# P1 of the feed-forward residual as seven smaller products in its own PSUM bank

## The chip, the cores and the metric

The kernel runs on one core of one Trainium2 chip. The metric is the device time of one execution in microseconds, as the median of several runs; lower is better. All numbers are fp32.

## The reference

A conditioned transformer block: two residual branches, each with a layer norm that is scaled and shifted by a vector of the condition, and gated by another. The tokens are 2 batches of 2048 with 512 features. The change lies in the last product, `hf @ ff_w2`.

```python
emb = jnp.dot(jax.nn.silu(t), ada_w) + ada_b
shift_msa, scale_msa, gate_msa, shift_mlp, scale_mlp, gate_mlp = jnp.split(emb, 6, axis=-1)
norm = _ln(x) * (1.0 + scale_msa[:, None]) + shift_msa[:, None]
h = jax.nn.gelu(jnp.dot(norm, ssm_w1) + ssm_b1, approximate=False)
ssm_out = jnp.dot(h, ssm_w2) + ssm_b2
x = x + gate_msa[:, None] * ssm_out
norm2 = _ln(x) * (1.0 + scale_mlp[:, None]) + shift_mlp[:, None]
hf = jax.nn.gelu(jnp.dot(norm2, ff_w1) + ff_b1, approximate=True)   # 512 -> 1024
ff_out = jnp.dot(hf, ff_w2) + ff_b2                                 # 1024 -> 512
x = x + gate_mlp[:, None] * ff_out
```

## The kernel before

The 4096 tokens are worked in 8 blocks of 512. First come the norms and the first branch (`ssm1`, `ssm2`) for all blocks, then the second branch in four pairs of blocks: `ff1` for a pair, then `ff2` for its two blocks one after the other. `weight_fw2(b)` prepares the second weight of the feed-forward for batch b: it loads it, multiplies it by the batch's gate and makes the combinations that the fast products need. It runs for batch 0 during the first branch and for batch 1 during the `ff1` of the third pair.

Every large product is done by the Strassen-Winograd scheme: a product of 2 by 2 quarters takes seven products, named P1 to P7, in place of eight. `first` and `second` make the operands of one side: four additions or subtractions (s0, s1, an in-place q21 or q12, and s2), and then P1 and P2 use quarters as they are, P5 uses s0, P6 uses s1, P7 the in-place one. In `ff2` the scheme is used twice. Of the seven outer products, P2, P3, P4, P5 and P7 are split again: each has seven inner products, which the code calls leaves. P1 and P6 are done whole by `plain`: 8 matmuls of 128 by 128 by 256 each, with 4 steps over the contraction.

The order on TensorE in one `ff2` block is written out: `plain("P1")`; then seven rounds over the inner products in the order of `LEAVES` (P1, P2, P6, P5, P7, P3, P4), each round one leaf of each of the five split products (10 matmuls of 128 by 128 by 128); `plain("P6")` stands between the first and the second round. Both plain products add up in one PSUM bank, `Y_SEED` (bank 2), which ScalarE seeds with the bias row (`seed`). VectorE adds PSUM results into `xt`, the block's residual rows, which are then stored. The leaves add up in banks of their own (`ROOMS`). Banks of name "y" are used by inner P1, P6, P7, P4, "x" by P2, "v" by P5 and P3; after round 0 ScalarE copies the "y" results to "x" (the room copies).

The code does not issue instructions directly. Each helper (`mm`, `tt`, `copy`, `act`, `dma`) adds an operation to `Plan`. `Plan.order` keeps TensorE's order as written, works back from it to the latest time at which each other operation is due, and lets a list scheduler choose the order on VectorE, ScalarE, GpSimd and the DMA queue; an operation marked "vg" may go to VectorE or GpSimd. It counts a PSUM bank as one cell: a write to a bank waits for all earlier reads of it by other engines.

Lines in the profile: L294 is the matmul of `mm`, L256 `tt` (all additions), L283 `copy`, L274 `act`, L316 the issue of a DMA. Names of tiles: `hidden` holds the gelu output (the token side of `ff2`), `near` and `far` the sums for the first and the second block of a pair, `fw` (fw2) the second weight and its combinations, `gb` the bias row times the gate, `rows` the residual rows, `ring` and `turned` the operands of `ff1`.

```python
LEAVES = ("P1", "P2", "P6", "P5", "P7", "P3", "P4")
LEAF_AT = {"P1": (0, 0), "P2": (0, 0), "P6": (0, 1), "P5": (1, 1), "P7": (1, 1), "P3": (0, 1), "P4": (1, 0)}
Y_SEED, V_SEED = 2, 1
ROOMS = {("P23", "y"): 0, ("P23", "x"): 3, ("P23", "v"): 4, ("P4", "y"): 5, ("P4", "x"): 6, ("P4", "v"): 7}
```

Of the kernel before, what the change touches and what calls it, by code (L numbers as in the profile page):

```python
# [12 lines left out]
ALU = mybir.AluOpType  # L13
# [185 lines left out]
def kernel(  # L199
# [17 lines left out]
    P = 128  # L217
# [33 lines left out]
    def tt(e, o, a, b, f):  # L251
        n, ps = cols(o), in_psum(a, b)
        cost = {"v": n / 0.96 + 70, "g": 2.12 * n + 145}
        plan.add(
            e,
            lambda E: E.tensor_tensor(o, a, b, f),  # L256
            [o],
            [a, b],
            cost,
            {"v": cost["v"] + 85, "g": cost["g"] + 45},  # L260
            "g" if ps else "vg",
        )
# [64 lines left out]
    def region(name, kb):  # L327
        t = const.tile([P, kb * 256], F32, tag=name, name=name)
        scratch.add(t.tensor.name)
        return t  # L330

    def kept(name, *shape):
        t = const.tile([P, *shape], F32, tag=name, name=name)
        scratch.add(t.tensor.name)
        return t
# [6 lines left out]
    def kb(t, at, n):  # L342
        return t[:, at * 256 : (at + n) * 256]

    def cut(t, form, **sizes):
        return t.rearrange(form, **sizes)

    turned_r, ring_r, hidden_r = region("turned", 28), region("ring", 27), region("hidden", 32)
    near_r, far_r, rows_r = region("near", 27), region("far", 27), region("rows", 16)
    fw2_r = region("fw2", 43)  # L350

    banks = []
    for n in range(8):
# [34 lines left out]
    gate_rows = {g: kb(hidden_r, 29, 1)[:, n * P : (n + 1) * P] for n, g in enumerate((2, 5))}  # L388
    gb2 = [kb(ring_r, 22, 2), kb(ring_r, 24, 2)]
    gate_sb = kb(near_r, 22, 2)  # L390
    gb5 = [kept(f"gb5_{b}", D) for b in range(B)]
    leaf_row = kept("leaf_row", 3, P)
    cols_t = kept("cols", 64)
    mods = {g: kept(f"mod_{g}", KD, B) for g in (0, 1, 3, 4)}
    half_t = kept("half", C)
    marks = [kept(f"marks_{n}", 60) for n in range(4)]
# [9 lines left out]
    def thirds(t):  # L406
        return [t[:, n] for n in range(3)]

    def first(q, s, e="vg", cuts=1):
        parts(e, s[0], q["21"], q["22"], ALU.add, cuts)  # L410
        parts(e, s[1], s[0], q["11"], ALU.subtract, cuts)
        parts(e, q["21"], q["11"], q["21"], ALU.subtract, cuts)
        parts(e, s[2], q["12"], s[1], ALU.subtract, cuts)
        return {"P1": q["11"], "P2": q["12"], "P3": s[2], "P4": q["22"], "P5": s[0], "P6": s[1], "P7": q["21"]}

    def second(q, s, e="vg", cuts=1):
# [6 lines left out]
    def parts(e, o, a, b, f, cuts):  # L423
        n = o.shape[1] // cuts
        for r in [slice(c * n, (c + 1) * n) for c in range(cuts)]:
            tt(e, o[:, r], a[:, r], b[:, r], f)
# [63 lines left out]
    def gate_bias(t, g_ps, row):  # L490
        load_row(t, row)
        tt("v", t, g_ps, t, ALU.mult)
        tt("vg", t[:, D // 2 :], t[:, D // 2 :], t[:, : D // 2], ALU.subtract)
# [218 lines left out]
    def seed(bank, row, part):  # L712
        half = row[:, part * (D // 2) : (part + 1) * (D // 2)]
        copy(pair(bank), half.unsqueeze(1).to_broadcast([P, 2, HT]))
# [66 lines left out]

    fw2_t = cut(kb(fw2_r, 0, 16), "p (k d) -> p k d", k=KH)
    fw2_s = cut(kb(fw2_r, 16, 12), "p (s k d) -> p s k d", s=3, k=KH // 2)
    fw2_l = cut(kb(fw2_r, 28, 15), "p (a s k d) -> p a s k d", a=5, s=3, k=2)

    def fw2_operands(make):
        first_level = lambda q, s, **kw: second(q, s, **kw) if make else second_names(q, s)

        wops = first_level(quarters_of_second(fw2_t, KH), thirds(fw2_s), cuts=2)
        pair_t = cut(kb(fw2_r, 28, 6), "p (s k q d) -> p s k q d", s=3, k=2, q=2)  # L790

        def views(w):
            v = cut(w, "p (h k) (q e d) -> p h k q e d", h=2, e=2, d=P)
            return {f"{h + 1}{e + 1}": v[:, h, :, :, e, :] for h in range(2) for e in range(2)}

        o23 = first_level(views(fw2_t[:, KH // 2 :, :]), thirds(pair_t))
        leaves = {p: {n: v[:, :, j, :] for n, v in o23.items()} for j, p in enumerate(("P2", "P3"))}
        lo12 = fw2_t[:, : KH // 2, D // 2 :]
        for j, (p, w) in enumerate((("P4", fw2_s[:, 2]), ("P5", fw2_s[:, 0]), ("P7", lo12))):
            q = {n: v[:, :, 0, :] for n, v in views(w).items()}  # L800
            leaves[p] = first_level(q, thirds(fw2_l[:, 2 + j]))
        return wops, leaves
# [4 lines left out]
    def weight_fw2(b, bank):  # L807
        plan.stage = f"weight_fw2 {b}"
        src = fw2.rearrange("(o n t p) d -> n o p t d", o=2, n=2, p=P)
        for n in range(2):  # L810
            for o in range(2):
                dma(fw2_t[:, 4 * n + 2 * o : 4 * n + 2 * o + 2], src[n, o], lead=100000.0)
        g = gate(5, b, bank)
        gate_bias(gb5[b], g, fb2)
        for k in range(KH):
            tt("v" if bank else "vg", fw2_t[:, k, :], fw2_t[:, k, :], g, ALU.mult)
        return fw2_operands(True)
# [122 lines left out]
    def ff2(s, blk, wops, leaf_wops):  # L940
# [3 lines left out]
        xt, F = x1_t[blk], D // 2  # L944
        for c in range(C):
            dma(xt[:, c], x1_d[i][:, c])
        row = gb5[i // PER_B]
        lo, hi = hC[:, blk, 0], hC[:, blk, 1]
        sums = cut(kb(sums_r[blk], 0, 12), "p (g s k t) -> p g s k t", g=2, s=3, k=2)
        hops = {}  # L950
        for g in range(2):
            r = slice(2 * g, 2 * g + 2)
            q = {"11": lo[:, r, :HT], "12": hi[:, r, :HT], "21": lo[:, r, HT:], "22": hi[:, r, HT:]}
            hops[g] = first(q, thirds(sums[:, g]))
        WL = 2 * P
        leaf_r = kb(sums_r[blk], 12, 15)
        r24, r35 = leaf_r[:, : 6 * WL], leaf_r[:, 6 * WL : 12 * WL]
        r7 = [leaf_r[:, (12 + n) * WL : (13 + n) * WL] for n in range(3)]
        hi_v = cut(hi, "p (g k) (q e t) -> p g k q e t", g=2, q=2, e=2)
        lo_v = cut(lo, "p (g k) (q e t) -> p g k q e t", g=2, q=2, e=2)  # L960
        eg = [(e, g, f"{e + 1}{g + 1}") for e in range(2) for g in range(2)]
        q24 = {n: hi_v[:, g, :, :, e, :] for e, g, n in eg}
        q35 = {n: sums[:, g, 0:3:2, :, e * P : (e + 1) * P] for e, g, n in eg}
        q7 = {n: lo_v[:, g, :, 1, e, :] for e, g, n in eg}
        o24 = first(q24, thirds(cut(r24, "p (s k q t) -> p s k q t", s=3, k=2, q=2)))
        o35 = first(q35, thirds(cut(r35, "p (s n k t) -> p s n k t", s=3, n=2, k=2)))
        o7 = first(q7, [cut(r, "p (k t) -> p k t", k=2) for r in r7])
        leaves = {
# [2 lines left out]
            "P3": {n: o[:, 1] for n, o in o35.items()},  # L971
            "P5": {n: o[:, 0] for n, o in o35.items()},
            "P7": o7,
        }

        seed(Y_SEED, row, 0)
        copy(banks[V_SEED][:, :P], row[:, F : F + P])
        tt("vg", leaf_row[:, 2], row[:, F + P :], row[:, F : F + P], ALU.subtract)
        quad_v = cut(banks[ROOMS["P4", "v"]], "p (n d) -> p n d", d=P)
        copy(quad_v[:, :3, :], leaf_row)  # L980

# [2 lines left out]
        def plain(p):  # L984
            for j in range(2):
                for k in range(KH // 2):
                    mm(
                        pair(Y_SEED)[:, j, :],
                        hops[k // 2][p][:, k % 2, j * P : (j + 1) * P],
                        wops[p][:, k, :],  # L990
                        False,
                        k == KH // 2 - 1,
                    )
# [22 lines left out]
                a = a.unsqueeze(1).to_broadcast(list(d.shape))  # L1016
            tt("v", d, a, d, ALU.add)

        plain("P1")
        add(xt[:, 0:2, :F], pair(Y_SEED))  # L1020
        for r, f in enumerate(LEAVES):
            t, e = LEAF_AT[f]
            on = ("P4", "P7", "P2", "P3", "P5") if last and r == 6 else ("P2", "P3", "P5", "P4", "P7")
            done = {p: leaf(p, f) for p in on}
            if r == 0:
                copy(rooms["P23", "x"][:, :2], rooms["P23", "y"][:, :2])
                copy(rooms["P4", "x"][:, :2], rooms["P4", "y"][:, :2])
                copy(rooms["P4", "x"][:, 2], seeded[:, 0])
                started.update({("P23", "x"), ("P4", "x")})
                plain("P6")  # L1030
                continue
            dests = {
                "P3": (X[:, 0, t, :, e, :], rooms["P23", BANK[f]][:, :2, :]),
                "P5": (X[:, :, t, 1, e, :], done["P5"]),
                "P4": (X[:, 1, t, 0, e, :], done["P4"]),
                "P7": (X[:, 1, t, :, e, :], done["P7"]),
            }
            for p in on:
                if p in dests:
                    add(*dests[p])  # L1040
            if r == 1:
                add(xt[:, 0:2, F:], pair(Y_SEED))
            if r == 2:
                d = cut(xt[:, 2:4, :], "p t (q d) -> p t q d", q=2)
                tt("v", d, pair(Y_SEED).unsqueeze(2).to_broadcast([P, 2, 2, F]), d, ALU.add)
            if last and r >= 4:
                for row_t in (t, 2 + t):
                    q = "sa"[row_t // 2]
                    if f == "P3":
                        dma(out_blk[i][:, row_t, :], xt[:, row_t, :], q)  # L1050
                    else:
                        cs = slice(e * P, (e + 1) * P)
                        dma(
                            out_blk[i][:, row_t].rearrange("p (q d) -> p q d", q=2)[:, :, cs],
                            cut(xt[:, row_t], "p (q d) -> p q d", q=2)[:, :, cs],
                            q,
                        )
# [210 lines left out]
```

## Time and profile before

| | |
|---|---|
| median of 3 runs | 572.83 us (572.78 to 573.93) |
| the profiled execution | 572.99 us |
| its span, first to last instruction | 571.2 us |
| granted TensorE clock | 0.999 |
| the four `ff1` stages begin at about | 216, 303, 391, 479 us |
| the `ff2` blocks of the four pairs begin at about | 257.9, 345.6, 434.2, 521.9 us |

PE is TensorE's matmuls and PEld its weight loads, DVE is VectorE, ACT ScalarE, POOL GpSimd. A timeline row gives the start, the length, engine and line, the operation, the tile written and the tiles read, the shape and the count of merged instructions, and in brackets the engine's idle time before it with what ended that. A row of a chain gives start, length and what worked. A row of groups ends with the busy time and the mean length in ns. Lengths of matmuls overlap, so the distance between starts is what a matmul takes.

### The profile page before, as it was taken

Reading aid. Unit: us, or ns where it says so; the run is one execution under the profiler, and the core shown is the slowest. Engines: PE = TensorE matmul, PEld = TensorE weight load, DVE = VectorE, ACT = ScalarE, POOL = GpSimd, SP = SyncE. Lnnn points to the kernel's source line nnn. Section 1 sums busy time; section 2 is a strip of 40 time slices with the busy share of each in tenths; the row PEclk is TensorE's granted clock in tenths of the full one; section 3 lists DMA queues with packets and bytes.
Section 4 is the critical chain, followed back from the end, with each engine's and each line's share of the span. In section 5 each row is a group of like instructions: output and inputs, shape, how many; then the busy total and the mean of one; then the engine's idle time right before and its main releaser. Section 6 shows DMA issues by size and latency. Waiting matters only on the chain.

```text
span 571.2 us, 9451 instructions
## 1 busy us (share of the span) xinstructions
PE 564.3 (99%) x3301; PEld 504.1 (88%) x3301; DVE 466.2 (82%) x881; ACT 242.9 (43%) x418; POOL 314.0 (55%) x403
## 2 busy tenths in 40 slices
PE   8999999999999999999999999999999999999997
PEld 4888888888888888889998888999888999888997
DVE  5695877778789788988985888998999986789846
ACT  3464947684856635574102455002365112335010
POOL 2893435979866586544701444803786743436620
PEclk9999999999999999999999999999999999999999
DMA  8953998998999889963316745228845043520022
GB/s 314 398 212 80 264 321 273 285 336 247 299 305 349 298 242 293 309 211 136 85 65 208 242 131 166 95 74 274 307 166 167 11 138 123 192 92 1 2 73 75
DMA packets 49659, 112.20 MB, mean 196 GB/s; under 512 B 5152, under 2 KB 9164, under 8 KB 48076
## 3 DMA queue, kind: packets, MB, share of 16 engines
q1 hardware_dynamic: 48848, 111.05, 58.9%
q10 hardware_dynamic: 764, 0.55, 0.3%
q8 instruction: 26, 0.43, 0.3%
q14 instruction: 21, 0.17, 0.1%
HBM read 73.69 MB, written 36.84 MB: 194 GB/s over the span
## 4 chain that ended last, share of the span: by engine, by line
PE 97%; DMA 1%; DVE 1%; ACTq 0%; issue 0%; DVEq 0%
PE bank L294 96%; DMA fw<-in_L_cond_ssm_b_dram 1%; DVE hidden L256 1%; PE bank L304 1%; ACTq L316 0%; DVE rows L256 0%; DVE turned L614 0%; DVE bank L464 0%; DVE mod L467 0%; DVEq L256 0%
## 5 line engine op out<-in xcount | busy, mean ns | idle before, releaser
L294 PE MATMUL bank<-turned,ring 128*128 128x256 f32 x896 | 205.0, 380 | 0.8 <-DVE hidden L256 0.6
L294 PEld LDWEIGHTS bank<-turned,ring 128*128 128x128 f32 x896 | 169.2, 190 | 25.2 <-DVE hidden L256 1.4
L256 DVE TENSOR_TENSOR hidden<-bank,hidden 128x512 f32<-128x512 f32 (+2 forms) x171 | 125.2, 756 | 43.4 <-PE bank L294 39.4
L256 DVE TENSOR_TENSOR rows<-bank,rows 128x256 f32<-128x256 f32 (+3 forms) x234 | 99.3, 457 | 29.5 <-PE bank L294 22.0
L294 PE MATMUL bank<-near,hidden 128*128 128x256 f32 x448 | 98.3, 379 | 0.0
L294 PEld LDWEIGHTS bank<-near,hidden 128*128 128x128 f32 x448 | 85.0, 190 | 11.8 <-POOL near L256 0.3
L294 PE MATMUL bank<-ring 128*128 128x256 f32 x336 | 82.2, 381 | 0.1
L294 PE MATMUL bank<-fw,hidden 128*128 128x128 f32 (+1 forms) x512 | 80.1, 301 | 0.0
L294 PEld LDWEIGHTS bank<-fw,hidden 128*128 128x128 f32 x512 | 72.9, 191 | 3.9
L283 ACT COPY bank<-bank 128x512 f32<-128x512 f32 (+2 forms) x66 | 31.7, 480 | 99.1 <-PE bank L294 98.7
L294 PEld LDWEIGHTS bank<-ring 128*128 128x128 f32 x336 | 63.2, 190 | 10.6 <-ACT bank L283 0.8
L294 PE MATMUL bank<-fw,far 128*128 128x128 f32 (+2 forms) x624 | 65.9, 286 | 0.0
L256 POOL TENSOR_TENSOR fw<-fw 128x256 f32<-128x256 f32 (+1 forms) x59 | 54.7, 945 | 17.7 <-DVE near L256 6.3
L294 PEld LDWEIGHTS bank<-fw,far 128*128 128x128 f32 (+1 forms) x624 | 59.8, 166 | 3.0 <-issue 1.2
L294 PE MATMUL bank<-fw,near 128*128 128x128 f32 (+1 forms) x432 | 59.5, 290 | 0.0
L256 POOL TENSOR_TENSOR turned<-turned 128x512 f32<-128x512 f32 (+1 forms) x44 | 49.4, 1139 | 16.6 <-ACT turned L274 6.4
L294 PEld LDWEIGHTS bank<-fw,near 128*128 128x128 f32 x432 | 54.9, 192 | 1.4
L274 ACT ACTIVATE hidden<-hidden,cols 128x512 f32<-128x512 f32 (+1 forms) x66 | 43.2, 707 | 29.2 <-DVE hidden L256 29.0
L256 POOL TENSOR_TENSOR hidden<-hidden 128x512 f32<-128x512 f32 (+1 forms) x31 | 37.9, 1224 | 26.7 <-ACT hidden L274 15.5
L274 ACT ACTIVATE turned<-turned,mod,mod 128x512 f32<-128x512 f32 x56 | 41.6, 803 | 8.7 <-DMA turned<-turned 4.5
L256 POOL TENSOR_TENSOR ring<-turned,ring 128x256 f32<-128x256 f32 x36 | 26.2, 731 | 25.6 <-PE bank L294 22.2
L256 POOL TENSOR_TENSOR ring<-turned 128x256 f32<-128x256 f32 x13 | 9.5, 728 | 50.2 <-PE bank L294 48.3
(103 smaller groups left out, 568.6 us busy)
## 6 DMA issues: line engine op xcount, KB each, us to landing
ring<-fw_parts SPq DMA_DIRECT2D x28, 512.0 KB
turned<-far SPq DMA_DIRECT2D x52, 256.0 KB
ring<-fw_parts SPq DMA_DIRECT2D x28, 384.0 KB
turned<-turned SPq DMA_DIRECT2D x32, 256.0 KB
rows<-x SPq DMA_DIRECT2D x32, 256.0 KB
out_dram<-rows SPq DMA_DIRECT2D x29, 256.0 KB
fw<-in_L_cond_ff_w_dram SPq DMA_DIRECT2D x12, 512.0 KB
fw_parts<-fw SPq DMA_DIRECT2D x21, 256.0 KB
```

The lines of the kernel that those rows point to most:

```text
L256: lambda E: E.tensor_tensor(o, a, b, f),
L274: lambda E: E.activation(o, a, func, bias=bias, scale=scale),
L283: plan.add("a", lambda E: E.copy(o, a), [o], [a], {"a": cost}, {"a": cost + 60})
L294: lambda E: E.matmul(o, lhsT, rhs, start=start, stop=stop, skip_group_check=True, **kw),
L304: lambda E: E.matmul(o, a, identity, start=start, stop=stop, is_transpose=True, skip_group_check=True),
```

## The change

P1 of `ff2` is split too. Its seven inner products are not spread over the rounds' banks but put together in the bank of P1 itself, whose four quarters of 128 columns are called `Y["11"]`, `Y["12"]`, `Y["21"]`, `Y["22"]`. `step(f, to)` is one inner product (two matmuls) into one quarter; `chain(r)` stands before round r, for r from 0 to 3:

- before round 0: inner P1 into 21 and P5 into 22; ScalarE copies 21 to 11, and 22 to SBUF (`spare`);
- before round 1: P6 is added to 21 and P2 to 11; VectorE writes 12 = 21 + `spare`; then the operand of inner P3 is made in place of that of P2 (`late`);
- before round 2: P7 is added to 21; VectorE writes 22 = 21 + `spare`;
- before round 3: P4 is added to 21, P3 to 12; VectorE adds the bank into `xt`.

`plain("P6")` moves from behind round 0 to behind round 3, and its additions into `xt` with it. ScalarE seeds only quarters 21 and 22; the bias row is stored as differences of quarters, made once for a batch in `weight_fw2` (with the third entry of `leaf_row`, so far made in each block). One bias row tile serves both batches in turn. `weight_fw2` makes a fourth set of inner weight operands, for P1, and `ff2` a set for the tokens. To make room, `first` may be called with two scratch tiles: it then leaves out s2, and `late` makes it in place of P2 after round 1 (for the tokens of P2/P4, P7 and P1).

```diff
@@ first
-        parts(e, s[2], q["12"], s[1], ALU.subtract, cuts)
+        if len(s) == 2:
+            s = [*s, q["12"]]
+        else:
+            parts(e, s[2], q["12"], s[1], ALU.subtract, cuts)
@@ fw2_operands
-    fw2_l = cut(kb(fw2_r, 28, 15), "p (a s k d) -> p a s k d", a=5, s=3, k=2)
+    fw2_l = cut(kb(fw2_r, 28, 18), "p (a s k d) -> p a s k d", a=6, s=3, k=2)
...
-        lo12 = fw2_t[:, : KH // 2, D // 2 :]
-        for j, (p, w) in enumerate((("P4", fw2_s[:, 2]), ("P5", fw2_s[:, 0]), ("P7", lo12))):
+        lo = fw2_t[:, : KH // 2]
+        for j, (p, w) in enumerate((("P4", fw2_s[:, 2]), ("P5", fw2_s[:, 0]), ("P7", lo[:, :, D // 2 :]), ("P1", lo[:, :, : D // 2]))):
@@ weight_fw2
-        gate_bias(gb5[b], g, fb2)
+        gate_bias(gb5, g, fb2)
+        for n in range(2):
+            lo, hi = [gb5[:, (2 * n + e) * P : (2 * n + e + 1) * P] for e in range(2)]
+            tt("vg", (hi, leaf_row[:, 2])[n], hi, lo, ALU.subtract)
@@ ff2
-        WL = 2 * P
-        leaf_r = kb(sums_r[blk], 12, 15)
-        r24, r35 = leaf_r[:, : 6 * WL], leaf_r[:, 6 * WL : 12 * WL]
-        r7 = [leaf_r[:, (12 + n) * WL : (13 + n) * WL] for n in range(3)]
+        rest = [kb(sums_r[blk], 12 + n, 1) for n in range(15)]
+        r24, r35 = kb(sums_r[blk], 12, 4), kb(sums_r[blk], 16, 6)
+        r7, r1, spare = rest[10:12], rest[12:14], rest[14][:, :P]
...
-        q7 = {n: lo_v[:, g, :, 1, e, :] for e, g, n in eg}
-        o24 = first(q24, thirds(cut(r24, "p (s k q t) -> p s k q t", s=3, k=2, q=2)))
+        q1, q7 = [{n: lo_v[:, g, :, q, e, :] for e, g, n in eg} for q in range(2)]
+        o1 = first(q1, [cut(r, "p (k t) -> p k t", k=2) for r in r1])
+        o24 = first(q24, [cut(r24, "p (s k q t) -> p s k q t", s=2, k=2, q=2)[:, n] for n in range(2)])
...
-        seed(Y_SEED, row, 0)
+        def late(o):
+            tt("vg", o["P2"], o["P2"], o["P6"], ALU.subtract)
+
+        copy(banks[Y_SEED][:, F:], row[:, :F])
         copy(banks[V_SEED][:, :P], row[:, F : F + P])
-        tt("vg", leaf_row[:, 2], row[:, F + P :], row[:, F : F + P], ALU.subtract)
...
-        plain("P1")
-        add(xt[:, 0:2, :F], pair(Y_SEED))
+        Y = {n: banks[Y_SEED][:, at * P : (at + 1) * P] for at, n in enumerate(("11", "12", "21", "22"))}
+
+        def step(f, to):
+            for k in range(2):
+                mm(Y[to], leaves["P1"][f][:, k, :], leaf_wops["P1"][f][:, k, :], False, f in ("P2", "P3", "P4") and k == 1)
+
+        def chain(r):
+            if r == 0:
+                step("P1", "21")
+                step("P5", "22")
+                copy(Y["11"], Y["21"])
+                copy(spare, Y["22"])
+            elif r == 1:
+                step("P6", "21")
+                step("P2", "11")
+                tt("v", Y["12"], Y["21"], spare, ALU.add)
+                late(o1)
+            elif r == 2:
+                step("P7", "21")
+                tt("v", Y["22"], Y["21"], spare, ALU.add)
+            elif r == 3:
+                step("P4", "21")
+                step("P3", "12")
+                add(xt[:, 0:2, :F], pair(Y_SEED))
+
         for r, f in enumerate(LEAVES):
+            chain(r)
...
-                plain("P6")
                 continue
+            if r == 1:
+                late(o24)
+                late(o7)
...
-            if r == 1:
+            if r == 3:
+                plain("P6")
                 add(xt[:, 0:2, F:], pair(Y_SEED))
-            if r == 2:
                 d = cut(xt[:, 2:4, :], "p t (q d) -> p t q d", q=2)
                 tt("v", d, pair(Y_SEED).unsqueeze(2).to_broadcast([P, 2, 2, F]), d, ALU.add)
```

More of the change, by code (lines that the diff above doesn't have):

```diff
@@ L349 @@
     near_r, far_r, rows_r = region("near", 27), region("far", 27), region("rows", 16)
-    fw2_r = region("fw2", 43)
+    fw2_r = region("fw2", 46)
     banks = []
@@ L390 @@
     gate_sb = kb(near_r, 22, 2)
-    gb5 = [kept(f"gb5_{b}", D) for b in range(B)]
+    gb5 = kept("gb5", D)
     leaf_row = kept("leaf_row", 3, P)
-    cols_t = kept("cols", 64)
+    cols_t = kept("cols", 48)
     mods = {g: kept(f"mod_{g}", KD, B) for g in (0, 1, 3, 4)}
@@ L946, in ff2 @@
             dma(xt[:, c], x1_d[i][:, c])
-        row = gb5[i // PER_B]
+        row = gb5
         lo, hi = hC[:, blk, 0], hC[:, blk, 1]
@@ L973, in ff2 @@
             "P7": o7,
+            "P1": o1,
         }
-        seed(Y_SEED, row, 0)
+        def late(o):
+            tt("vg", o["P2"], o["P2"], o["P6"], ALU.subtract)
+        copy(banks[Y_SEED][:, F:], row[:, :F])
         copy(banks[V_SEED][:, :P], row[:, F : F + P])
-        tt("vg", leaf_row[:, 2], row[:, F + P :], row[:, F : F + P], ALU.subtract)
         quad_v = cut(banks[ROOMS["P4", "v"]], "p (n d) -> p n d", d=P)
```

## The prediction, made before the changed kernel ran

> **What bounds the kernel now.** I read the page's busy line and its chain first, then the chain of waits in order of time, then timelines of PE, ACT, DVE and POOL around the ff2 blocks. Busy line and chain shares:
>
> ```profile
> PE 564.3 (99%) x3301; PEld 504.1 (88%) x3301; DVE 466.2 (82%) x881; ACT 242.9 (43%) x418; POOL 314.0 (55%) x403
> ...
> PE 97%; DMA 1%; DVE 1%; ACTq 0%; issue 0%; DVEq 0%
> ```
>
> The chain that ended last runs through TensorE for 97% of the span. The chain in order of time, ff half (start, length, what):
>
> ```profile
> 256.95 87.70 PE bank L294 x540
> 344.65 0.01 issue
> 344.66 82.52 PE bank L294 x516
> ...
> 427.19 1.22 DVE hidden L256
> ...
> 431.20 1.99 PE bank L294 x8
> ...
> 433.21 87.70 PE bank L294 x540
> ...
> 520.92 45.75 PE bank L294 x344
> ```
>
> From 257 us on PE pauses in one place only, around 430 us, where it waits for VectorE's ff1 evictions while VectorE and GpSimd also make the second batch's ff weights. So matmul time taken out of ff2 comes out of the total, if nothing else becomes late. The PE timeline of ff2 at the start of the second pair of blocks (start, us, records):
>
> ```profile
> 345.60 4.06 PE L294 MATMUL bank<-fw,hidden 128*128 128x256 f32 x20
> 349.50 1.06 PE L294 MATMUL bank<-fw,near 128*128 128x128 f32 x8
> 350.39 1.06 PE L294 MATMUL bank<-fw,hidden 128*128 128x128 f32 x8
> 351.29 3.62 PE L294 MATMUL bank<-fw,near 128*128 128x256 f32 x16
> 354.74 0.61 PE L294 MATMUL bank<-fw,hidden 128*128 128x128 f32 x4
> ...
> 356.97 4.63 PE L294 MATMUL bank<-fw,near 128*128 128x128 f32 x40
> 361.44 0.61 PE L294 MATMUL bank<-fw,hidden 128*128 128x128 f32 x4
> ```
>
> Each fp32 matmul shows as two records. The x20 row is plain P1 (16 records, 256 wide) and the first leaf; the x16 row is plain P6; between them stand the five leaves of round 0. Durations overlap, so I go by starts: P6 takes 354.74 - 351.29 = 3.45 us, 0.2156 a record; forty narrow records take 361.44 - 356.97 = 4.47 us, 0.1118 a record. A leaf (4 records) is 0.447 us, a round of five 2.235.
>
> **The PE term.** Plain P1 goes: 8 matmuls, 16 records, 3.45 us. Seven leaves of two matmuls come: 28 records, 28 x 0.1118 = 3.13. That is 0.32 us less per block, 2.56 for the eight blocks. It is the only term on the path by right; the rest costs nothing as long as it is hidden.
>
> A rule of the chip notes speaks against it. The row first:
>
> ```profile
> L294 PEld LDWEIGHTS bank<-fw,near 128*128 128x128 f32 x432 | 54.9, 192 | 1.4
> ```
>
> There are 28 weight loads for 16. The Trainium skill ("TensorE: Matmul & The Clock Gate", Back-to-back issue gap) says that the spacing of narrow matmuls is set by the weight load too, about 81 ns at 128 columns where the moving data alone would need 56. By an estimate from that ratio a 128-wide record would cost about 0.7 of a 256-wide one, and the change would lose about 1 us a block. The x40 row disagrees: a load of 192 ns and a pitch of 111.8 mean that loads overlap, and the narrow record costs 0.1118/0.2156 = 0.52 of the wide one.
>
> **What moves.** With T the start of a block, PE had: P1 to T+3.45, round 0 to 5.69, P6 to 9.14, rounds 1 to 6 to 22.55. It now has: P1 and P5 steps to 0.89, round 0 to 3.13, P6 and P2 steps to 4.02, round 1 to 6.26, the P7 step to 6.71, round 2 to 8.94, P4 and P3 steps to 9.84, round 3 to 12.07, plain P6 to 15.52, rounds 4 to 6 to 22.23. So round 1 wants its operands 5.1 us sooner, round 2 4.7, round 3 4.7; rounds 4 to 6 stand as before. That is the real price: two covers of 3.45 us are gone from the front. The next items ask what becomes late.
>
> Copies on ScalarE. Rows after round 0, and two at the next block's edge (T = 368.15):
>
> ```profile
> 345.75 2.56 ACT L274 ACTIVATE hidden<-hidden,cols 128x512 f32<-128x512 f32 x4 [0.58 <-DVE hidden L256]
> 350.15 0.36 ACT L283 COPY bank<-bank 128x256 f32<-128x256 f32 x1 [1.84 <-PE bank L294]
> 351.54 0.64 ACT L283 COPY bank<-bank 128x256 f32<-128x256 f32 x2 [1.04 <-PE bank L294]
> ...
> 368.28 0.27 ACT L283 COPY bank<-gb 128x128 f32<-128x128 f32 x1 [0.30 <-DVE rows L256]
> ```
>
> The room copies end 0.25 + 0.64 = 0.89 us after round 0's last leaf (351.29 to 352.18); plain P6 hid them. Now the P6 and P2 steps and the first two leaves of round 1 (0.89 + 0.89) stand before the first reader of that room, so 0.9 us remain. The two new copies (of 11 from 21, and of 22 to SBUF) at 0.27 each start about 0.25 after T+0.89 and are over by T+1.7; the P6 step wants the bank at T+3.13. ScalarE's four gelus of the other block lie here at a pair's start, 0.64 each; a copy waits for one at most, which leaves 0.8. The bias copy at 368.28 ends at T+0.40 and P5's leaf wants it at T+1.79. The seed of the bank shrinks from 512 to 256 columns. ScalarE: nothing on the path.
>
> Handoffs in the bank. The 12 sum (VectorE) may run from T+4.02 to the P7 step at 6.26, the 22 sum from 6.71 to 8.94, the add into x from 9.84 to 12.07. The two sums are 128x128 from PSUM; they lie between 0.28 (the 128x128 row of 438.41 below, from SBUF) and 0.37 (half of the 368.91 row below, two PSUM adds, one of them wider); I take 0.3, nearer to the same width. The add is the 0.69 of the 349.26 row below. With about 0.25 of hop each has 1.3 to 1.7 us to spare.
>
> Operands on VectorE and GpSimd, second pair (T = 345.60):
>
> ```profile
> 344.48 1.28 POOL L256 TENSOR_TENSOR near<-hidden,near 128x512 f32<-128x512 f32 x1
> 345.72 1.29 POOL L256 TENSOR_TENSOR near<-near,hidden 128x512 f32<-128x512 f32 x1
> ...
> 347.81 0.68 DVE L256 TENSOR_TENSOR near<-near 128x512 f32<-128x512 f32 x1
> 348.41 0.41 DVE L256 TENSOR_TENSOR near<-near,hidden 128x256 f32<-128x256 f32 x1
> 349.26 0.69 DVE L256 TENSOR_TENSOR rows<-bank,rows 128x512 f32<-128x512 f32 x1 [0.43 <-PE bank L294]
> ...
> 368.91 0.74 DVE L256 TENSOR_TENSOR rows<-bank,rows 128x128 f32<-128x128 f32 x2
> ```
>
> Round 1 needs the first of these (s2 of the second half of the contraction, done at T+0.2), round 2 the s1 of each product, the next three (done at T+1.4, 2.9 and 3.2). They are wanted from T+4.47 and T+6.71: 3.5 us of room. Into it go three 128x256 operations for P1 (0.41 on VectorE each); out of it go the 0.69 add, now after round 3, and the s2 of two products, made later in place of P2. The fourth new operation (P2 minus P6) has from T+4.02 to 9.4. The tightest edge is the next block's round 0: its fourth leaf overwrites the bank that the 368.91 adds empty (done at T+1.50); plain P1 gave it until T+4.8, now it is T+2.23. It holds by 0.6 with a hop. At an ordinary edge I put the wait at nothing; if one contended operation lands there it costs up to a microsecond.
>
> **The third pair** is the thin place: its weights are made in the ff1 before it. PE, VectorE, GpSimd, and busy time by stage (PE, PEld, DVE, ACT, POOL):
>
> ```profile
> 431.20 1.99 PE L294 MATMUL bank<-turned,ring 128*128 128x256 f32 x8 [0.58 <-DVE hidden L256]
> ...
> 434.15 4.06 PE L294 MATMUL bank<-fw,hidden 128*128 128x256 f32 x20
> ```
>
> ```profile
> 434.97 1.74 DVE L256 TENSOR_TENSOR near<-near 128x512 f32<-128x512 f32 x1
> ...
> 438.41 0.28 DVE L256 TENSOR_TENSOR leaf_row<-gb 128x128 f32<-128x128 f32 x1
> ...
> 440.95 1.08 DVE L256 TENSOR_TENSOR fw<-fw 128x256 f32<-128x256 f32 x3
> ```
>
> ```profile
> 434.87 1.29 POOL L256 TENSOR_TENSOR near<-near,hidden 128x512 f32<-128x512 f32 x1
> 437.73 0.73 POOL L256 TENSOR_TENSOR fw<-fw 128x256 f32<-128x256 f32 x1 [1.57 <-DVE near L256]
> ...
> 443.99 1.27 POOL L256 TENSOR_TENSOR fw<-fw 128x512 f32<-128x512 f32 x1 [4.71 <-DVE near L256]
> 446.02 0.73 POOL L256 TENSOR_TENSOR fw<-fw 128x256 f32<-128x256 f32 x1 [0.76 <-DVE fw L256]
> ```
>
> ```profile
> 345.60:390.00 44.40, 44.40 (x339) 42.74 (x338) 39.09 (x84) 8.68 (x17) 16.94 (x16) 1.00 0.36 117
> 390.00:434.00 44.00, 43.41 (x204) 37.55 (x203) 40.76 (x60) 19.96 (x33) 33.92 (x35) 1.00 0.71 236
> ```
>
> Here T = 434.15. The change adds four weight operations of 256 (0.73 on GpSimd) and a 128x128 on the bias row, and wants P1's s0 of weights and of tokens by T+0.45, both s1 by T+3.13, the weights' and tokens' P7 part by T+6.26, P4's by T+8.94. In order of need that is four 256-wide operations before T+3.1, 2.9 us if GpSimd makes them all. GpSimd's work up to 436.16 (its 434.87 row) is wanted only by rounds 1 and 2 and can slide by about that: to 439.1, against T+6.71 = 440.86. From 436 to 446 GpSimd idles 1.57 + 4.71 + 0.76 = 7.0 us, so there is room behind it. What can go wrong is order: VectorE's first operation after T took 1.74 us for 0.68, beside GpSimd. I allow 0.3 us here, between -0.58 (the old pause falls away in the new order) and +1.5 (the 1.06 of one such collision and a hop of 0.25 on top of a slack used up). The first batch's weights are made over 40 us before their use; their extra operations cost nothing.
>
> The DMAs are the same in number and size. The bias row's second load now waits for the first batch's last read of it, a whole ff1 earlier.
>
> **The sum.** 572.83 - 2.56 + 0.3 = 570.6. The profiled execution took 572.99 (span 571.2 and 1.8 around it), 0.16 above the median; by it the sum is 570.7. The pitch of 40 rows leaves about 0.1 either way.
>
> **Rivals.** (1) Slower: P1's weight leaves stand last in the third pair's queue. The last weight operation ended at 446.75, T+12.60, as it was wanted only in round 6. If P1's last two come behind it on GpSimd (2 x 0.73), the P4 step, due at T+8.94, starts at T+14.06 + 0.25: PE waits 5.4 us, and the time is 572.83 - 2.56 + 5.4 = 575.7. It decides the sign once P1's s2 lands after T+12.4 (a wait of 3.7). For it: the two engines were 40.76 and 33.92 busy of 44.00 in the ff1 before. Against it: the queues are ordered by when PE wants a result, and the gaps of 7.0 us. Chance 0.10. (2) No change: one bank handoff in each block arrives about 0.3 us late, 8 x 0.3 = 2.4, time 572.7. For it: a collision adds 1.06 to an operation (434.97), and spares are 0.6 to 1.7. The Trainium skill ("SBUF — State Buffer", Who interferes with whom) has such a VectorE operation block until GpSimd's reading one is done; the 434.97 row agrees. Against it: the collision must hit the same handoff each time, and adds from PSUM read one SBUF operand only. Chance 0.14. (3) Narrow records cost more here than in the x40 row, as the weight-load rule would have it: with loads of 192 ns in a row, 28 x 0.192 = 5.38 for 3.45, 1.93 x 8 = 15.4 more, 588. The x40 row speaks against it; chance 0.02. (4) Waits of 1.2 to 3 us in all, at the third pair and a block edge or two, each of the size of the 1.06 collision: 571.5 to 573.3; chance 0.12.
>
> **How the numbers follow.** The forecast, 569.6 (the old pause gone) to 571.4, has 0.62. About 0.2% of the time, 1.15 us, can be told from no change: faster is under 571.68, slower over 573.98. Faster: the forecast and a part of (4), 0.66. Same: (2) and most of (4), 0.21. Slower: (1), (3) and a little of (2), 0.13. The range goes from 569.6 to 573.4, which takes in (4) and most of (2).
>
> **What would show it.** Right: 28 records of about 0.112 us pitch for plain P1's 16, in four groups before rounds 0 to 3; plain P6 after round 3; a block of 22.2 us; no pause of PE in ff2 but at most one below a microsecond near 430 to 445. Wrong: PE idle before a step in the P1 bank, released by VectorE or ScalarE, in every block (2); PE idle before the P7 or P4 step near 440 to 448, released by a weight operation (1); a narrow pitch over 0.12 (3).

## The result and the profile after

The changed kernel takes 571.24 us in the median of 6 runs (571.16 to 572.0), beside 573.02 for the kernel before (572.78 to 573.93, 6 runs). The ratio is 0.9968 with a 95% interval of 0.9955 to 0.998: 1.8 us faster. The forecast was 2.2 us faster (570.6 from 572.83), in a range of 569.6 to 573.4. The profiled execution took 571.29 us, its span 569.5.

Busy line and chain shares of the page after:

```profile
PE 562.3 (99%) x3397; PEld 505.0 (89%) x3397; DVE 472.8 (83%) x892; ACT 245.6 (43%) x434; POOL 350.7 (62%) x444
```

PE has 96 records more (8 blocks x 12) and 2.0 us less of busy time. VectorE gains 6.6 us and GpSimd 36.7: the queues were ordered anew, and 41 of the 52 additional operations went to GpSimd, the slower of the two (0.73 us for a 128x256 addition that VectorE makes in 0.41). The chain in order of time, same part as before:

```profile
257.07 87.05 PE bank L294 x564
...
344.13 85.30 PE bank L294 x556
429.44 0.49 issue
429.93 1.97 PE bank L294 x8
...
431.91 26.44 PE bank L294 x216
458.35 0.07 issue
458.42 3.36 PE bank L294 x28
461.79 0.04 issue
461.83 58.06 PE bank L294 x320
...
519.90 45.09 PE bank L294 x368
```

The first piece is 87.05 us where it was 87.70: 0.65 less for two blocks. The pause near 430 is still there, and two new breaks stand at 458 and 461, in block 5. PE in block 2 (second pair, T = 345.07), then in block 5 from the last two leaves of round 0 on, and VectorE there (its rows at 457.26 and 460.88 end with the operands of the P6 and the P7 step):

```profile
345.07 0.61 PE L294 MATMUL bank<-fw,hidden 128*128 128x128 f32 x4
345.52 0.61 PE L294 MATMUL bank<-fw,near 128*128 128x128 f32 x4
345.96 0.61 PE L294 MATMUL bank<-fw,hidden 128*128 128x128 f32 x4
346.41 1.06 PE L294 MATMUL bank<-fw,near 128*128 128x128 f32 x8
347.30 1.06 PE L294 MATMUL bank<-fw,hidden 128*128 128x128 f32 x8
348.20 0.61 PE L294 MATMUL bank<-fw,near 128*128 128x128 f32 x4
```

```profile
457.29 1.06 PE L294 MATMUL bank<-fw,hidden 128*128 128x128 f32 x8
458.42 0.68 PE L294 MATMUL bank<-fw,far 128*128 128x128 f32 x4
...
460.73 1.81 PE L294 MATMUL bank<-fw,hidden 128*128 128x128 f32 x12
462.43 2.65 PE L294 MATMUL bank<-fw,far 128*128 128x128 f32 x20
```

```profile
457.26 1.01 DVE L256 TENSOR_TENSOR far<-far,hidden 128x512 f32<-128x512 f32 x2
...
460.88 0.89 DVE L256 TENSOR_TENSOR hidden<-hidden 128x256 f32<-128x256 f32 x1
```

In block 2 the P1 and P5 steps, round 0 and the P6 step follow each other without a break: 28 records from 345.07 to 348.20, 0.112 each. In block 5 the P6 step starts 1.13 after the row ahead of it, where eight records take 0.89. The last four of the twelve records at 460.73 are the P7 step, and that row takes 1.70 where twelve records take 1.34. Both steps start within 0.15 us of the end of their operand on VectorE (458.27 and 461.77). The rest of the loss lies right behind: the P6 step takes 0.52 for 0.45, and the twenty records of round 2 take 2.49 for 2.24. The sum is 0.24 + 0.07 + 0.36 + 0.26 = 0.93.

From the PE timeline's starts, us in each stage (ff1 before a pair, then the pair; the last pair to its last record):

| | before | after |
|---|---|---|
| first pair | 45.08 | 44.42 |
| ff1, second pair | 42.64, 45.08 | 42.64, 44.42 |
| ff1, third pair | 43.47, 45.08 | 43.35, 45.35 |
| ff1, fourth pair | 42.64, 44.97 | 42.64, 44.31 |
| start of ff2 to last record | 308.95 | 307.14 |

Three pairs gain 0.66 each, the full price of two blocks. The third loses 0.27 instead, so 0.93 are missing there, and all of it in block 5. The question for the experiments is what takes it.

### The profile page after: what moved, and what is told of

Read it like the earlier page. It is cut to its first block, busy times and chain, and to the rows that moved or that the text cites. A ratio compares the mean times of both kernels' runs of the same rounds, so it can differ in the third digit from the quotient of the medians.

```text
span 569.5 us, 9767 instructions
## 1 busy us (share of the span) xinstructions
PE 562.3 (99%) x3397; PEld 505.0 (89%) x3397; DVE 472.8 (83%) x892; ACT 245.6 (43%) x434; POOL 350.7 (62%) x444
## 4 chain that ended last, share of the span: by engine, by line
PE 97%; DMA 1%; DVE 0%; SPq 0%; issue 0%; DVEq 0%
PE bank L294 97%; DMA fw<-in_L_cond_ada_w_dram 1%; PE bank L304 0%; SPq L316 0%; DVE rows L256 0%; DVE turned L617 0%; DVE bank L467 0%; DVE mod L470 0%; DVEq L256 0%
## 5 line engine op out<-in xcount | busy, mean ns | idle before, releaser
L294 PEld LDWEIGHTS bank<-turned,ring 128*128 128x128 f32 x896 | 169.2, 190 | 25.3 <-POOL near L256 0.9
L294 PE MATMUL bank<-fw,hidden 128*128 128x128 f32 x640 | 83.9, 275 | 0.0
L283 ACT COPY bank<-bank 128x512 f32<-128x512 f32 (+2 forms) x74 | 33.7, 456 | 105.5 <-PE bank L294 104.8
L294 PEld LDWEIGHTS bank<-fw,hidden 128*128 128x128 f32 x640 | 78.5, 192 | 0.9 <-DVE hidden L256 0.2
L256 POOL TENSOR_TENSOR turned<-turned 128x512 f32<-128x512 f32 (+1 forms) x49 | 54.4, 1122 | 16.2 <-ACT turned L274 7.2
L274 ACT ACTIVATE hidden<-hidden,cols 128x512 f32<-128x512 f32 (+1 forms) x66 | 44.7, 710 | 29.4 <-DVE hidden L256 29.1
L256 POOL TENSOR_TENSOR hidden<-hidden 128x512 f32<-128x512 f32 (+1 forms) x34 | 42.2, 1244 | 23.2 <-ACT hidden L274 15.3
L256 POOL TENSOR_TENSOR fw<-fw 128x256 f32<-128x256 f32 (+1 forms) x57 | 52.0, 929 | 7.3 <-DVE fw L256 4.4
L294 PEld LDWEIGHTS bank<-fw,near 128*128 128x128 f32 x416 | 53.7, 192 | 1.4
L256 POOL TENSOR_TENSOR ring<-turned,ring 128x256 f32<-128x256 f32 x39 | 28.8, 743 | 23.4 <-PE bank L294 20.4
L274 ACT ACTIVATE hidden<-bank,cols 128x256 f32<-128x256 f32 x62 | 25.8, 469 | 16.1 <-PE bank L294 16.0
```

What stands on the lines that cost most here:

```text
L274: lambda E: E.activation(o, a, func, bias=bias, scale=scale),
L283: plan.add("a", lambda E: E.copy(o, a), [o], [a], {"a": cost}, {"a": cost + 60})
L294: lambda E: E.matmul(o, lhsT, rhs, start=start, stop=stop, skip_group_check=True, **kw),
```

## The experiments

Every run is compared with runs of the kernel before that were made beside it. The span from the start of ff2 to the last record is used beside the ratio, because the start of ff2 itself lies anywhere from 257.8 to 258.8 in these 13 profiles; the eleven that start from the changed kernel have the same operations in the same order on TensorE, VectorE, ScalarE and GpSimd up to 240 us, and spread just as far. Without a wait it would be 305.5. The load theory: in the third pair VectorE and GpSimd make the second batch's weights besides, and block 5's operands come late. The order theory: the two covers that left the front are the price by themselves. One caution holds for every run: an edit makes the plan anew, so it can change the order of operations that it doesn't name.

| run | ratio (95%) | ff1 before the third pair | third pair | start of ff2 to last record |
|---|---|---|---|---|
| changed kernel | 0.9968 (0.9955 to 0.998) | 43.35 | 45.35 | 307.14 |
| p6_moved | 1.0007 (0.9999 to 1.0016) | 42.85 | 45.35 | 309.36 |
| no_p1_weights | 0.994 (0.9925 to 0.9955) | 42.65 | 44.99 | 306.08 |
| no_p1_tokens | 0.9949 (0.9935 to 0.9962) | 42.66 | 44.42 | 305.58 |
| no_weights_b1 | 0.9941 (0.9928 to 0.9955) | 42.63 | 44.42 | 305.50 |
| whole_in_45 | 0.9965 (0.9953 to 0.9978) | 43.42 | 45.08 | 306.94 |
| p1_tokens_gpsimd | 0.9999 (0.999 to 1.0008) | 42.66 | 47.95 | 309.05 |
| copies_x4 | 1.0027 (1.0017 to 1.0036) | 42.64 | 45.94 | 310.49 |
| p1_tokens_block4 | 0.9975 (0.9966 to 0.9984) | 42.65 | 46.30 | 307.39 |
| p1_tokens_split | 1.0061 (1.0047 to 1.0076) | 42.72 | 51.09 | 312.31 |
| weights_gpsimd | 0.9981 (0.9972 to 0.9989) | 42.66 | 46.88 | 307.97 |
| whole_in_45_gpsimd | 0.9949 (0.9935 to 0.9963) | 42.64 | 45.08 | 306.17 |

**The move of P6 alone** (on the kernel before):

```diff
                 started.update({("P23", "x"), ("P4", "x")})
-                plain("P6")
                 continue
...
-            if r == 1:
+            if r == 3:
+                plain("P6")
                 add(xt[:, 0:2, F:], pair(Y_SEED))
-            if r == 2:
```

> The kernel before, with plain P6 and its adds moved behind round 3 and nothing else: no new operand, no new handoff, the same matmuls. Rounds 1 to 3 come 3.45 us sooner after the start of a block. Load theory (block 5's operands come late because VectorE and GpSimd make the second batch's weights besides): the time stays at 573.0, within 0.3, and PE waits in ff2 for 0.3 us at most in all. Order theory (the two covers that left the front are the price by themselves): PE waits about 0.9 us in block 5, near 458 to 464 us, and the time is 573.9.

The time was 573.55 beside 573.48, and the interval of the ratio contains 1. Block 5 has no large wait, so the order alone is not what costs 0.93. But every pair takes 45.33 or 45.35, 0.25 more than before (45.22 for 44.97 in the last): 1.0 in all, more than the 0.3 that the load theory allowed. The pause in the third ff1 is 0.62 shorter, and 4 x 0.25 - 0.62 = 0.4 is the difference of the spans (309.36 for 308.95). The timeline of PE and ScalarE shows 0.15 of the 0.25 in the pair's first block; the other 0.10 is at the same place in its second:

```profile
350.77 1.50 PE L294 MATMUL bank<-fw,hidden 128*128 128x128 f32 x12
352.12 1.21 PE L294 MATMUL bank<-fw,near 128*128 128x128 f32 x8
353.16 1.06 PE L294 MATMUL bank<-fw,hidden 128*128 128x128 f32 x8
```

```profile
351.92 0.64 ACT L283 COPY bank<-bank 128x256 f32<-128x256 f32 x2 [1.04 <-PE bank L294]
```

The row at 352.12 takes 1.04 to the next one, where eight records take 0.89. Its last four are P5's leaf, which reads the room that the copies fill; they end at 352.56 and are the last releaser in the trace. With P6 gone from between round 0 and round 1 and nothing in its place, the copies are no longer quite hidden. In the changed kernel the P6 and P2 steps (0.89) stand there, and PE shows no wait for the copies.

**Operations left out of the changed kernel.** Four weight operations for P1 of the second batch; the four token operations for P1 of every block; all of the second batch's weight work:

```diff
-            leaves[p] = first_level(q, thirds(fw2_l[:, 2 + j]))
+            leaves[p] = (second_names if p == "P1" and b else first_level)(q, thirds(fw2_l[:, 2 + j]))
```

> The changed kernel without the four weight operations for P1 of the second batch (its leaves read the quarters as they lie). Load theory: 0.2 to 0.6 of the 0.9 us lost in the third pair come back, 570.6 to 571.0. Order theory: they change nothing in block 5, 571.2.

```diff
-        o1 = first(q1, [cut(r, "p (k t) -> p k t", k=2) for r in r1])
+        o1 = {"P1": q1["11"], "P2": q1["12"], "P3": q1["12"], "P4": q1["22"], "P5": q1["11"], "P6": q1["21"], "P7": q1["21"]}
...
-                late(o1)
```

> The changed kernel without the four token operations for P1 in every block (its leaves read raw quarters). If the waits before the P6 and P7 steps of block 5 are for just these operations (the last releasers there), they go and the time is 570.3. If they are a sign of general lateness, the wait moves to the next late operand: 570.6 to 571.0. If a bank handoff is late, 571.2.

```diff
         if 2 * s == PER_B:
-            ff = weight_fw2(1, None)
```

> The changed kernel without all of the second batch's weight work (the second batch uses the weights of the first). Load theory: the third pair takes the 44.42 us of the others and the pause of about 0.7 us in the ff1 before it goes too: 571.24 - 0.93 - 0.7 = 569.6. Order theory: the pause goes, the 0.93 stays: 570.5.

Without the second batch's weights the third pair takes 44.42 like the others, and the pause is gone: 305.50, no wait left. The 570.00 are 0.4 above the expected 569.6, as was the kernel before beside them (573.48 for 573.02). Leaving out the tokens' operations alone does nearly the same (305.58, and 570.52 us), so the wait did not move to another operand, as I had thought it might. Leaving out the four weight operations gives back the pause and 0.36 in the pair, and the time, 570.11 us, is below what either theory said; block 5 keeps one wait, for the P7 step's operand:

```profile
461.31 0.71 PE L294 MATMUL bank<-fw,hidden 128*128 128x128 f32 x4 [0.30 <-POOL hidden L256]
```

So neither load makes block 5 late alone: with either taken away, block 5 is on time or nearly so. VectorE and GpSimd by stage, changed kernel (ff1, then third pair) and the kernel without the second batch's weights (same two; columns PE, PEld, DVE, ACT, POOL):

```profile
389.50:432.85 43.35, 42.84 (x199) 36.99 (x198) 40.74 (x60) 19.80 (x33) 33.27 (x34) 1.00 0.72 234
432.85:478.20 45.35, 45.23 (x369) 43.89 (x368) 42.33 (x91) 10.09 (x22) 30.57 (x33) 1.00 0.26 82
```

```profile
389.32:431.95 42.63, 42.62 (x198) 37.00 (x197) 33.38 (x50) 20.15 (x34) 20.31 (x24) 1.00 0.67 207
431.95:476.38 44.43, 44.43 (x370) 43.60 (x368) 40.08 (x85) 9.56 (x21) 25.57 (x23) 1.00 0.28 90
```

The weights are 7.4 us of VectorE and 13.0 of GpSimd in the ff1, and 2.3 and 5.0 in the pair.

**P1 whole in the third pair**, as in the kernel before, with its weights of the second batch made after that pair (shortened; `whole` is true for blocks 4 and 5):

```diff
-        for r, f in enumerate(LEAVES):
-            chain(r)
+        if whole:
+            plain("P1")
+            add(xt[:, 0:2, :F], pair(Y_SEED))
+        for r, f in enumerate(LEAVES):
+            if not whole:
+                chain(r)
...
+                if whole:
+                    plain("P6")
                 continue
```

> The changed kernel, but in the third pair (blocks 4 and 5) P1 is one whole product in front and P6 behind round 0, as in the kernel before; the second batch's weight operands for P1 are made after that pair. Load theory: the third pair takes the 45.08 us of before instead of 45.35, and the ff1 ahead of it loses its pause of 0.7 (42.65 instead of 43.35), so 571.24 - 0.27 - 0.7 = 570.3. Order theory: the pair takes 45.08 and the pause stays, 571.0.

The time was 571.31. The pair takes the expected 45.08. The pause stays at 43.42, which speaks for the order theory on that point alone: a weight operation of VectorE still stands ahead of the ff1's last evictions. Here the same place in VectorE's queue, in this kernel, in the changed one and in the kernel before:

```profile
424.96 0.93 DVE L256 TENSOR_TENSOR fw<-fw 128x256 f32<-128x256 f32 x1 [0.37 <-POOL fw L256]
425.82 7.86 DVE L256 TENSOR_TENSOR hidden<-bank,hidden 128x1024 f32<-128x1024 f32 x9
```

```profile
425.01 0.93 DVE L256 TENSOR_TENSOR near<-near,hidden 128x256 f32<-128x256 f32 x1
425.87 7.87 DVE L256 TENSOR_TENSOR hidden<-bank,hidden 128x1024 f32<-128x1024 f32 x9
```

```profile
426.33 0.93 DVE L256 TENSOR_TENSOR fw<-fw 128x256 f32<-128x256 f32 x1 [0.42 <-POOL fw L256]
```

The row of nine evictions mixes two shapes: three write 128x1024, since they add one bank to two places, and take 1.21 us; six write 128x512 in 0.69. In all they take VectorE 7.86 us, 0.87 each in the mean, while PE finishes a bank every 0.86. What stands ahead of them can't be caught up. In the kernel before it was a weight operation too.

**That one operation** sent to GpSimd, in block 4 alone:

```diff
-        o1 = first(q1, [cut(r, "p (k t) -> p k t", k=2) for r in r1])
+        o1 = first(q1, [cut(r, "p (k t) -> p k t", k=2) for r in r1], e="g" if i == 4 else "vg")
```

> The changed kernel with the first three token operations for P1 on GpSimd in block 4 alone. In the changed kernel VectorE makes one of them at 425 us, right ahead of nine ff1 evictions that take it 0.87 us each while PE delivers one every 0.86. If that one operation is the pause of 0.7 us, the ff1 before the third pair falls from 43.35 to 42.65 and the time to 570.5, with block 5's waits as they are. If VectorE is short of time over the whole stage, another operation takes the place and the time stays at 571.2.

The pause is gone (42.65), so it is that operation. But the pair takes 46.30, 0.95 more than in the changed kernel: the 0.7 came back as waits of block 5, and the time is 571.38. What was expected of block 5 was wrong. VectorE ends the operand of block 5's P6 step 69.0 us after the start of the third ff1, for 68.8 in the changed kernel; PE waits 0.94 for it, for 0.24, and 0.24 for another operand just before. As long as that operand comes no sooner, taking the pause away gains nothing.

**More of the work on GpSimd**: the same edit with `e="g"`, with `e="gv"[blk]`, and the inner weights of the second batch (`first_level(..., e="g" if b else "vg")`).

> The changed kernel with the first three token operations for P1 of each block on GpSimd only (0.73 us each for 0.41 on VectorE). If VectorE alone is what is short in the third pair, its 45.35 us fall to 44.6 and the time to 570.5. If the two engines are short together, it stays at 571.2 or rises by up to 0.6. The other pairs stay at 44.42 in both cases.

> The changed kernel with the first three token operations for P1 on GpSimd in the first block of each pair and on VectorE in the second. Both losses of the third pair should shrink: no pause in the ff1 (42.65), and block 5 waits less than 0.9 us, since a 128x256 operation takes 0.41 on VectorE for 0.73; 569.6 to 570.5. If VectorE is the short one in block 5, its waits grow and the time is 571 or more.

> The changed kernel with the second batch's inner weight operations for P1, P4, P5 and P7 (sixteen of 128x256) on GpSimd only. Around blocks 4 and 5 GpSimd idles about 10 us while it waits for VectorE's results, and eight of the sixteen stand on VectorE there (0.41 each, up to 1 us beside GpSimd). If VectorE's share of the weight work is what makes block 5 late, the third pair falls from 45.35 to 44.6 or less and the time to 570.5 or less. If the two are short together, it stays or rises as with the token operations: 571.2 to 573.

The times were 573.45, 576.86 and 572.16. Each takes the pause away and pays more in the third pair: 47.95, 51.09 and 46.88. The other three pairs stay at 44.42 in all of them. So VectorE is not short alone. In the split kernel not all of the 6.67 us are waits: after the longest one the granted clock is 0.5 from 467.0 to 470.4 us, and a narrow record takes 0.213 there for 0.112, which is about 1.7. In the kernel with the weights on GpSimd, PE also waits 0.2 before block 4's P4 step for a weight operation, the place that the first rival named. In the split kernel VectorE even idles while GpSimd makes block 5's operands one after the other (VectorE, then GpSimd, then one of PE's waits in the whole run):

```profile
455.77 1.05 DVE L256 TENSOR_TENSOR far<-far,hidden 128x256 f32<-128x256 f32 x1
459.72 0.30 DVE L256 TENSOR_TENSOR bank<-bank,far 128x128 f32<-128x128 f32 x1 [2.89 <-PE bank L294]
...
463.82 1.08 DVE L256 TENSOR_TENSOR rows<-bank,rows 128x256 f32<-128x256 f32 x3 [2.02 <-PE bank L294]
464.82 0.87 DVE L256 TENSOR_TENSOR hidden<-hidden 128x256 f32<-128x256 f32 x1
```

```profile
457.91 1.26 POOL L256 TENSOR_TENSOR far<-far,hidden 128x512 f32<-128x512 f32 x1
...
461.70 1.26 POOL L256 TENSOR_TENSOR hidden<-hidden 128x512 f32<-128x512 f32 x1
```

```profile
PE bank L294 <- DVE hidden L256: 2.0, 1, 2.0
```

VectorE's next operations in its fixed order add up banks that PE has not finished, and PE waits for GpSimd's operands. The operand at 464.82, for which PE then waits 2.0 us, stands behind such an addition at 463.82. So what is short there is not one engine's time: the order makes the engines wait for each other in turn. That the same holds in the changed kernel, with its 0.93, is argued from this and not shown. Why the plan chose this order wasn't tried.

**The spare of the bank copies**, which the prediction put at 1.4 us, or 0.8 at a pair's start:

```diff
-                copy(Y["11"], Y["21"])
-                copy(spare, Y["22"])
+                for _ in range(4):
+                    copy(Y["11"], Y["21"])
+                    copy(spare, Y["22"])
```

> The changed kernel with the two bank copies ahead of round 0 done four times over, which changes no value. Three more pairs take 3 x 0.53 = 1.6 us on ScalarE. If the copies end 1.4 us before the P6 step wants the bank (2.08 before a pair's second block less 0.8 at a pair's start, where the gelus lie in between), PE waits 0.1 to 0.4 us in second blocks and up to 0.9 in first blocks, 1 to 4 us in all: 572.2 to 575. If the spare is larger than read, 571.2.

The time was 574.86. PE starts the P6 step 0.36 late in each second block and 0.45 to 0.71 late in first blocks. PE and ScalarE in block 3 (a second block), and PE's waits in the whole run:

```profile
371.86 1.06 PE L294 MATMUL bank<-fw,hidden 128*128 128x128 f32 x8
373.11 0.71 PE L294 MATMUL bank<-fw,far 128*128 128x128 f32 x4 [0.20 <-ACT far L283]
```

```profile
370.77 0.25 ACT L283 COPY bank<-bank 128x128 f32<-128x128 f32 x1
...
372.79 0.27 ACT L283 COPY far<-bank 128x128 f32<-128x128 f32 x1
```

```profile
PE bank L294 <- ACT near L283: 1.9, 4, 0.5
PE bank L294 <- ACT far L283: 0.8, 4, 0.2
```

Eight copies end at 373.06, and the step starts at 373.11. Two would have ended at 371.33, 1.4 before the 372.75 at which eight records after 371.86 are over. The spare was as read for a pair's second block. In block 2, at a pair's start, it was 1.4 as well and not 0.8: two copies end at 348.33 there, the step is due at 349.77, and it comes 0.70 late, not 0.36, with a room copy among the eight.

The edit gives VectorE and GpSimd no work and takes none from them, yet the pause in the third ff1 is gone here too (42.64): in this plan nothing stands ahead of VectorE's nine evictions. So the pause depends on the order that the plan happens to choose, and not on the amount of work alone.

**P1 whole in the third pair, with the inner weights of the second batch on GpSimd**:

```diff
-else first_level)(q, thirds(fw2_l[:, 2 + j]))
+else first_level)(q, thirds(fw2_l[:, 2 + j]), e="g" if b else "vg")
```

> The kernel with P1 whole in the third pair, and the second batch's inner weight operations for P4, P5 and P7 on GpSimd only. The one weight operation that VectorE made ahead of the nine evictions goes: no pause of 0.7 in the ff1 before the pair, the pair as before at 45.08, 571.3 - 0.7 = 570.6. If something else takes its place, 571.3.

570.58, ratio 0.9949 (0.9935 to 0.9963): the shortest of the kernels that compute everything. The pause is gone and the pair is at 45.08, as expected. Its chain in the ff half has no wait left:

```profile
257.76 87.05 PE bank L294 x564
344.83 87.05 PE bank L294 x564
431.90 87.71 PE bank L294 x540
519.62 45.09 PE bank L294 x368
```

The interval overlaps that of the changed kernel, and the two were not run side by side; in the profiles it is 0.97 shorter from the start of ff2 on (306.17 for 307.14).

## Why the prediction was right, and where it was not

*The PE term* was right: 0.32 a block was read from pitches, 0.33 was measured in the six blocks of three pairs. The narrow pitch stayed at 0.112, and the third rival (weight loads) is out: 12 more loads a block cost nothing that the trace shows. Eight blocks at 0.33 less the 0.81 of the third pair below make 1.83; the spans from the start of ff2 differ by 1.81.

*The copies on ScalarE* were right. In block 2 they run from 346.22 to 346.77, which is T+1.15 to T+1.70. They wait for PE alone; the gelu ahead of them ended at 345.94:

```profile
346.22 0.25 ACT L283 COPY bank<-bank 128x128 f32<-128x128 f32 x1 [0.28 <-PE bank L294]
346.50 0.27 ACT L283 COPY near<-bank 128x128 f32<-128x128 f32 x1
```

The fourfold copies measured their spare. The move of P6 alone showed that the room copies need a cover: without the 0.89 of the two steps, PE is 0.15 late.

*The handoffs* were right. The sums take 0.28 to 0.30 for the 0.3 taken, and no pair but the third has a wait. The second rival, a handoff late in every block, did not happen, nor did a collision at an ordinary edge. Two readings on the way were off without effect: round 3 itself starts 3.8 us sooner (9.84 for 13.61), not 4.7, and the tightest edge had 2.23 - 1.50 - 0.25 = 0.5 left with a hop, not 0.6.

*The third pair* is the step that was mis-sized. It allowed 0.3 and bounds of -0.58 to 1.5; against the kernel before, the ff1 gave 0.12 back and block 5 took 0.93, so 0.81 in all, within the bounds. The old pause was worth 0.83 by starts (43.47 for 42.64), not the 0.58 of its idle time. The place was wrong too: the argument was made for block 4, where rounds 1 to 3 run without a break, and P1's weights were in time, so the first rival did not happen. The step counted it as free to push later work back, and the work for block 5 moved back. Its first operand in the changed kernel, in the second and in the third pair:

```profile
353.54 1.96 POOL L256 TENSOR_TENSOR far<-hidden 128x512 f32<-128x512 f32 x2 [0.42 <-ACT turned L274]
```

```profile
449.77 1.27 POOL L256 TENSOR_TENSOR far<-hidden 128x512 f32<-128x512 f32 x1
```

Its first operand in the kernel before, in the same two pairs:

```profile
352.52 1.28 DVE L256 TENSOR_TENSOR far<-hidden 128x512 f32<-128x512 f32 x2
```

```profile
446.71 2.51 POOL L256 TENSOR_TENSOR far<-hidden 128x512 f32<-128x512 f32 x2
```

That is T+8.5 in the second pair and T+16.9 in the third (T = 432.85); before, it was T+6.9 and T+12.6. Block 5 wants its P6 step's operand at T+25.3 and gets it at T+25.4, with 0.15 more to PE's start. The fourth rival named the third pair and waits of this kind, but 1.2 to 3 us of them and a time from 571.5 on; less was lost, and the 571.24 lie in the forecast's own range. Two loads were weighed one at a time, each against its own idle time; they met in the block behind.

## What to carry to other kernels

A stage that is bound by TensorE passes on what is taken out of it, as long as the operands keep up; read the pitch of the new shape from a stretch of the trace that has it in a row, and the sum holds to a hundredth. When covers are moved from the front of a block, look for the stage in which the helper engines have another job, and follow the work that is pushed back until it is done: the late one may be the block after. Where helper engines wait for each other in a fixed order, moving work to the engine that seems idle can make the wait longer.

## What the runs showed that I had not expected

At the end of ff1 VectorE needs 0.87 us in the mean for an eviction while PE fills a bank in 0.86, so one operation of 0.93 ahead of nine evictions costs PE 0.7 us; in the kernel before a weight operation stood in that place. Without the pause the time need not fall, since block 5's operand was late by itself. A VectorE addition of 128x256 in SBUF took 0.41 alone and 0.93 beside a GpSimd operation. And the start of ff2 differs by up to 1 us between profiles of the same early program, which is more than half of the gain that was measured.
